# A cross-attention block with a feed-forward layer: the feature order of the key/value input, and the order of the first loads

## The chip, the cores and the metric

The kernel runs on one core of one Trainium2 chip. The metric is the time of one execution on the device, in microseconds (us). Before the change three runs gave 788.25 us as the median (787.9 to 791.28).

The engines are called by their names in the profile: PE (TensorE, matmuls; PEld is its loading of weights), DVE (VectorE), ACT (ScalarE), POOL (GpSimd) and SP (SyncE, which here only issues transfers). A name with a q (SPq, ACTq, POOLq) is the engine's instruction queue, where it waits and issues.

## The reference

For each of 16 batches `b`, with `x[b]` and `ctx[b]` both 128 x 1024 in float32:

```
h   = layernorm(x)
Q   = h @ Wq + bq                 # 1024 x 1024, 32 heads of 32
K   = ctx @ Wk + bk               # 1024 x 256, 8 heads of 32
V   = ctx @ Wv + bv               # 1024 x 256
w   = softmax(Q K^T / sqrt(32))   # 4 query heads share one key/value head
x   = x + (w V) @ Wo + bo
x   = x + scale * (ei(layernorm(x)) @ kernel)   # 1024 x 1024, entries 0 or 1; ei scales the last 205 features by -4
```

The change concerns K and V alone: sums over the 1024 features of `ctx` with `Wk` and `Wv`. The order in which these features are summed is free, as long as `ctx` and the weights use the same one.

## The kernel before

The batches go in 8 groups of two (`GB = 2`). PE multiplies with 128 features at a time on the partitions, so each operand is cut into `NC = 8` chunks of 128 features. The weights `Wv` and `Wk` (each 1024 x 256, 1 MB) are read once into `wv_sb` and `wk_sb`, laid out as [partition, chunk, column]. `Wq` and `Wo` come again and again in pieces of 512 KB.

`ctx[b]` comes with rows on the partitions and is wanted with features on the partitions. DVE's transpose (`turn_ctx`, line 349) turns blocks of 32 x 32 only, so `load_ctx` (line 152) makes four transfers of 128 KB per batch: transfer k puts features 256k to 256k+255 of all 128 rows on the 32 partitions 32k to 32k+31, in runs of 1 KB, four per partition. Two transposes of 128 x 512 elements then give the two halves of `cT`: the first half has chunks 0 to 3, the second 4 to 7. Before the change feature 256k + 32c + f stands on partition 32k + f of chunk c, and a transpose reads its 32 x 32 blocks as 32 adjacent elements of a partition. `load_by_quadrants` (line 161) brings the weights in the same order: one transfer per quadrant of 32 partitions and per cut of chunks, in runs of 1 KB (one row of 256 columns): 12 for `Wv` (cuts at chunks 2 and 4), 8 for `Wk` (a cut at 4).

The transfers of the start are dealt round-robin to three issuing engines (SP, ACT, POOL) in the order `ctx0`, `Wv`, `ctx1`, `Wk`; then SP alone issues `x0`, `x1` (line 169), `bo` (line 201) and the first eight pieces of `Wq` (line 225). The tile framework gives the transfers of SP and ACT eight completion semaphores in turn, so that a transfer waits in its queue until the one issued eight before it has landed.

The order of the work is written out by hand on the host: a `Stream` holds generators of PE work, and a list of later events. In the first stage, PE's order is `v` of batch 0, `v` of batch 1 (`prep_v`, 16 matmul records each), `k` of both (`prep_k`, 32), the transposes of the normalized `x` (`tp_x`), then the plain `q` product. DVE's order is: two transposes of `ctx0`, two of `ctx1`, the two additions `v + bv` (line 412), `bqs` (line 852), and `norm_x(0)`, `norm_x(1)`: two `bn_stats` each (line 283), their aggregate, a power on POOL (line 291) and one scaling (line 292). An engine's instructions run strictly in order.

In the next stage (group 0's attention with the preparation of group 1) DVE also has the softmax (row maxima L580, division L596), sums of pieces of `Wq` (L790), the transposes of the next group's `ctx` (L349), its normalizations and `v` additions. PE needs from it above all `cT` for `k` and the divided `p` for its transposes `tpp` (L601). From group 1 on `x` too goes through DVE's transposes (L371), and the output projection's partial sums are read by DVE (L676) before PE may go on in their PSUM buffer. In each later group four transposes of `ctx` are due.

Of the kernel before, what the change touches and what calls it, by code (L numbers as in the profile page):

```python
# [9 lines left out]
FP = mybir.dt.float32  # L10
# [7 lines left out]
P = 128  # L18
# [64 lines left out]
def kernel(  # L83
# [16 lines left out]
    nc = tc.nc  # L100
# [7 lines left out]
    NC = D // P  # L108
    XB = 3
    TB = 4  # L110
    GB = 2
# [9 lines left out]
    work = ctx.enter_context(tc.tile_pool(name="work", bufs=1))  # L121
# [8 lines left out]
    wk_sb = const.tile([P, NC, KV], FP, name="wk_sb")  # L130
    wv_sb = const.tile([P, NC, KV], FP, name="wv_sb")
# [13 lines left out]
    NB = P // 32  # L145

    def load_ctx(b, queues=(nc.sync,)):
        c_t = work.tile([P, NB, NC, 32], FP, tag="ctx", name=f"ctx{b}", bufs=2)
        src = key_value[b].rearrange("(t r) (k c f) -> k r t (c f)", r=32, k=NB, c=NC)
        for k in range(NB):  # L150
            dst = c_t[k * 32 : (k + 1) * 32].rearrange("r t c f -> r t (c f)")
            queues[k % len(queues)].dma_start(out=dst, in_=src[k])
        cs[b] = c_t

    def load_by_quadrants(dst, w, queues, *cuts):

        src = w.rearrange("(k c f) n -> k f c n", k=NB, f=32)
        n = 0
        for lo, hi in zip((0,) + cuts, cuts + (NC,)):
            for k in range(NB):  # L160
                queues[n % len(queues)].dma_start(
                    out=dst[k * 32 : (k + 1) * 32, lo:hi], in_=src[k][:, lo:hi]
                )
                n += 1

    def load_x(b, tag="row"):

        x_t = work.tile([P, D], FP, tag=tag, name=f"xn{b}", bufs=2)
        nc.sync.dma_start(out=x_t, in_=x[b])
        xns[b] = x_t  # L170
# [10 lines left out]
            )  # L181

    three = (nc.sync, nc.scalar, nc.gpsimd)
    load_ctx(0, three)
    load_by_quadrants(wv_sb, Wv, (nc.scalar, nc.gpsimd, nc.sync), 2, 4)
    load_ctx(1, three)
    load_by_quadrants(wk_sb, Wk, (nc.scalar, nc.gpsimd, nc.sync), 4)
    load_x(0)  # L190
    load_x(1)
    ident = const.tile([P, P], FP, name="ident")
    make_identity(nc, ident)
# [88 lines left out]
    def half_stats(stats, src, k):  # L282
        nc.vector.bn_stats(stats[:, k], src[:, k * HALF : (k + 1) * HALF])

    def normalize(dst, src, stats, name):
        mv = small.tile([P, 2], FP, tag="mv", name=f"mv_{name}")
        nc.vector.bn_aggr(mv, stats)
        ve = small.tile([P, 1], FP, tag="ve", name=f"ve_{name}")
        nc.vector.tensor_scalar_add(ve, mv[:, 1:2], EPS)
        rstd = small.tile([P, 1], FP, tag="rstd", name=f"rs_{name}")  # L290
        nc.gpsimd.tensor_tensor(rstd, ve, minus_half, ALU.pow)
        nc.vector.tensor_scalar(dst, src, mv[:, 0:1], rstd, ALU.subtract, ALU.mult)
# [24 lines left out]
    def new_stats(name):  # L317
        return small.tile([P, D // HALF, 6], FP, tag="stats", name=f"st_{name}")
# [9 lines left out]
    HC = NC // 2  # L328
# [15 lines left out]
    def turn_ctx(b, h):  # L344
        grp, j = b // GB, b % GB
        if (grp, h) not in cTs:
            cTs[grp, h] = work.tile([P, HC, T], FP, tag="tT", name=f"cT{grp}_{h}", bufs=TB)
        src = cs.pop(b) if h == 1 else cs[b]
        nc.vector.transpose(  # L349
            cTs[grp, h][:, :, j * S : (j + 1) * S].rearrange("p c (t n) -> p t c n", t=NB),  # L350
            src[:, :, h * HC : (h + 1) * HC],
        )

    rows = {}
# [21 lines left out]
    def prep_ctx(grp, *us):  # L376

        for n, at in enumerate(us if grp < NGRP else ()):
            stream.later(at, lambda n=n: turn_ctx(grp * GB + n % GB, n // GB))
# [7 lines left out]
    def norm_x(b):  # L387
        stats = new_stats(f"a{b}")
        for k in range(D // HALF):
            half_stats(stats, xns[b], k)  # L390
        normalize(xns[b], xns[b], stats, f"a{b}")
# [432 lines left out]
    with tc.manual_schedule():  # L824
        stream = Stream()
# [18 lines left out]
        for j in range(GB):  # L844
            for h in range(2):
                turn_ctx(j, h)
            stream.add(prep_v(0, [j]))
        stream.add(prep_k(0))
        for j in range(GB):
            load_ctx(GB + j)  # L850
        stream.run(0.0, lambda: len(stream.queue) > 1)
        nc.vector.tensor_scalar_mul(bqs, bqT, scale)
        for j in range(GB):
            norm_x(j)

        def sums_of_wo():
            def inputs():
# [57 lines left out]
        for grp in range(NGRP):  # L915
# [5 lines left out]
            if first:  # L921
                stream.add(
                    once(prep_ctx, nxt, 12.5, 13.5),
                    between(plain(1), 9, sums_of_wq, 0),
                    once(sums_of_wq, 1),
                    once(turn_ctx, nxt * GB, 1),
                    once(turn_ctx, nxt * GB + 1, 1),
                    once(norms, nxt, 5.0, 10.0),
# [33 lines left out]
            if not more:  # L962
                for q in range(2 * NA):
                    b, a = grp * GB + q % GB, q // GB
# [6 lines left out]
            for q in range(2 * NA):  # L971
                b, a = grp * GB + q % GB, q // GB
# [66 lines left out]
```

## Time and profile before

| | |
|---|---|
| median of 3 runs | 788.25 us |
| profiled execution, its time | 788.44 us |
| its span in the profile | 786.7 us |
| PE busy | 767.2 us (98%) |
| DVE, ACT, POOL busy | 486.3, 322.4, 112.2 us |
| mean share of 16 DMA engines, slices of the first 255 us | 0.6 to 0.9 and more |
| transposes of `ctx`, L349 | 32 of 699 ns, 22.1 us |
| steady groups | one every 93.8 us |

The span runs from the first instruction to the last; 1.8 us of the time lie outside it. The chain that ended last is PE for 88% of the span, DVE for 4%, DMA for 2%. In the windows of 94 us from 151 us to 621 us PE is busy for all of each window, so what happens on the other engines there shows in the time only if PE comes to wait. The waits that PE has are few and lie in the first 150 us; the prediction shows them.

In a row of the timeline the columns are start, duration, engine, line, operation, written and read tile, count of merged instructions, and in brackets the idle time before the first with what ended it. In a row of the stage table they are the stage and its length, then busy time and count of instructions for PE, PEld, DVE, ACT and POOL, granted clock of PE, share of the DMA engines and GB/s (or PE's alone, where that engine was asked for). A matmul's record counts its pass through the array, which overlaps the next one's.

### The profile page before, as it was taken

To read this page: it belongs to the slowest core of one execution; us is meant where nothing else is said; L and a number is where in the kernel's file an instruction comes from. 1 tells how busy PE (TensorE), PEld (TensorE's weight loads), DVE (VectorE), ACT (ScalarE), POOL (GpSimd) and SP (SyncE) were. 2 spreads that over 40 slices of the span, in tenths; PEclk is the share of its full clock that TensorE was granted. 3 is DMA by queue.
4 is the path that set the end of the run, shared out by engine and by line. 5 is a ranking of instruction groups with operands and counts; after the bars stand their busy time and mean duration, and the time that the engine had idled before them with its cause. 6 is when DMAs were issued, how large, how long until landed. Compare 5 with 4: busy or idle time off the path is not lost.

```text
span 786.7 us, 13740 instructions
## 1 busy us (share of the span) xinstructions
PE 767.2 (98%) x5008; PEld 571.6 (73%) x5008; DVE 486.3 (62%) x886; ACT 322.4 (41%) x1261; POOL 112.2 (14%) x142
## 2 busy tenths in 40 slices
PE   5998999999999999999999999999999999999997
PEld 4886884589746997479864898558984699556476
DVE  2158647756766567566774667856676666765552
ACT  0254764444334443344433444334434445575100
POOL 4154703020010102010020200202001010103000
PEclk9999999999999999999999999999999999999999
DMA  9999799988698776978778785987869657763802
GB/s 248 344 309 303 273 341 392 268 226 282 216 322 230 238 235 232 306 204 261 239 240 271 213 272 188 305 257 202 266 209 328 206 192 238 250 202 104 264 27 81
DMA packets 99268, 192.42 MB, mean 245 GB/s; under 512 B 8240, under 2 KB 57456, under 8 KB 99200
## 3 DMA queue, kind: packets, MB, share of 16 engines
q1 hardware_dynamic: 97568, 189.43, 74.9%
q0 software_dynamic: 528, 1.12, 0.6%
q10 hardware_dynamic: 1104, 0.98, 0.6%
q8 instruction: 40, 0.66, 0.3%
q14 instruction: 28, 0.23, 0.1%
HBM read 161.09 MB, written 30.41 MB: 243 GB/s over the span
## 4 chain that ended last, share of the span: by engine, by line
PE 88%; DVE 4%; DMA 2%; issue 2%; ACT 1%; POOL 1%; SPq 0%; POOLq 0%; DVEq 0%
PE f L323 14%; PE o_u L662 13%; PE q_u L451 12%; PE o_v L662 7%; PE tpp L601 7%; PE q_v L451 6%; PE k L323 6%; PE v L323 6%; PE sc L568 4%; PE av L611 4%; PE q L323 3%; PE o_c L662 3%; PE q_c L451 3%; DVE p L596 1%; DMA piece<-o 1%
## 5 line engine op out<-in xcount | busy, mean ns | idle before, releaser
L584 ACT ACTIVATE p<-sc,negm 128x128 f32<-128x128 f32 x512 | 181.1, 368 | 134.4 <-DVE negm L580 72.5
L603 ACT COPY pt<-tpp 128x512 f32<-128x512 f32 x128 | 74.6, 591 | 148.1 <-PE tpp L601 147.9
L580 DVE TENSOR_REDUCE negm<-sc 128x4 f32<-128x512 f32 x128 | 86.8, 680 | 59.3 <-PE sc L568 59.3
L584 ACT ACTIVATION_READ_ACCUMULATOR p<-sc,negm 128x1 f32 x512 | 105.5, 206 | 0.0
L323 PE MATMUL f<-wf_sb,x2l 128*128 128x512 f32 x256 | 104.3, 408 | 0.0
L323 PE MATMUL f<-wf_sb,x2h 128*128 128x512 f32 x256 | 100.5, 393 | 0.0
L596 DVE TENSOR_TENSOR p<-p,inv 128x512 f32<-128x512 f32 x128 | 90.9, 710 | 4.4
L451 PE MATMUL q_u<-t,piece 128*128 128x128 f32 x672 | 81.3, 275 | 0.0
L601 PEld LDWEIGHTS tpp<-ident,p 128*128 128x128 f32 x512 | 62.2, 141 | 24.9 <-issue 16.8
L601 PE MATMUL tpp<-ident,p 128*128 128x128 f32 x512 | 76.4, 274 | 3.7 <-DVE p L596 3.5
L451 PEld LDWEIGHTS q_u<-t,piece 128*128 128x128 f32 x672 | 78.0, 192 | 0.1
L180 POOL TENSOR_TENSOR x<-x,bo_b 128x256 f32<-128x256 f32 x64 | 53.6, 862 | 155.7 <-DMA x<-in_x_dram 155.7
L323 PE MATMUL v<-wv_sb,cT 128*128 128x256 f32 x256 | 62.2, 393 | 9.0 <-DMA wv_sb<-in_L_xattn_Wv_dram 7.1
L662 PE MATMUL o_v<-piece,s 128*128 128x512 f32 x128 | 60.3, 598 | 0.5 <-DVE x L676 0.5
L323 PEld LDWEIGHTS v<-wv_sb,cT 128*128 128x128 f32 x256 | 48.4, 197 | 15.8 <-DVE cT L349 9.4
L662 PE MATMUL o_u<-piece,s 128*128 128x512 f32 x128 | 59.2, 594 | 0.6 <-DVE x L676 0.6
L323 PE MATMUL k<-cT,wk_sb 128*128 128x256 f32 x256 | 58.3, 380 | 1.0 <-DVE cT L349 1.0
L662 PE MATMUL o_u<-piece,yT 128*128 128x512 f32 x128 | 58.6, 599 | 0.0
L323 PEld LDWEIGHTS f<-wf_sb,x2l 128*128 128x128 f32 x256 | 48.2, 188 | 10.6 <-issue 1.1
L323 PEld LDWEIGHTS k<-cT,wk_sb 128*128 128x128 f32 x256 | 47.9, 190 | 10.2 <-issue 2.6
L323 PEld LDWEIGHTS f<-wf_sb,x2h 128*128 128x128 f32 x256 | 48.2, 188 | 9.6 <-issue 0.5
L568 PEld LDWEIGHTS sc<-kT,qT 32*128 32x128 f32 x1024 | 31.4, 186 | 25.8 <-issue 25.8
(86 smaller groups left out, 935.1 us busy)
## 6 DMA issues: line engine op xcount, KB each, us to landing
piece<-o SPq DMA_DIRECT2D x64, 512.0 KB, 5.0
piece<-q SPq DMA_DIRECT2D x56, 512.0 KB, 5.1
piece<-in_L_xattn_Wq_dram SPq DMA_DIRECT2D x50, 512.0 KB, 5.2
piece<-in_L_xattn_Wo_dram SPq DMA_DIRECT2D x48, 512.0 KB, 4.6
xn<-in_x_dram SPq DMA_DIRECT2D x16, 512.0 KB, 6.8
x<-in_x_dram SPq DMA_DIRECT2D x16, 512.0 KB, 4.6
ctx<-in_ctx_dram SPq DMA_DIRECT2D x60, 128.0 KB, 6.6
out_dram<-x SPq DMA_DIRECT2D x15, 512.0 KB, 2.7
```

Source lines behind the costliest of these rows:

```text
L180: lambda cut=cut: nc.gpsimd.tensor_add(x_t[:, cut], x_t[:, cut], bo_b[:, cut]) and None,
L323: nc.tensor.matmul(mm, lhsT=lhsT, rhs=rhs, start=k == 0, stop=k == n - 1)
L451: nc.tensor.matmul(mm if part is None else mm[:, part], lhsT=lhsT, rhs=rhs, start=start and n == k == 0, stop=k == len(some) - 1, skip_gro ...
L568: nc.tensor.matmul(tiles[i][:, g], lhsT=qT[rows, g], rhs=kT[rows, a, cols], start=True, stop=True,)
L580: nc.vector.tensor_reduce(negm, tile_, AX.X, ALU.max, negate=True)
L584: nc.scalar.activation(p[:, g], tile_[:, g], AF.Exp, bias=negm[:, g : g + 1], accum_out=total[:, g : g + 1],)
L596: nc.vector.tensor_mul(p, p, inv.unsqueeze(2).to_broadcast([P, NG, S]))
L601: nc.tensor.transpose(tp[:, g], p[:, g], ident)
L603: nc.scalar.copy(pt, tp)
L611: nc.tensor.matmul(mm[i * HD : (i + 1) * HD], lhsT=vs[b][:, h * HD : (h + 1) * HD], rhs=pts[i], start=True, stop=True,)
L662: nc.tensor.matmul(mm, lhsT=lhsT[:, 2 * k + c], rhs=w[:, c], start=start and k == c == 0, stop=k == c == 1, skip_group_check=True,)
```

## The change

The features of K's and V's input are taken in another order: feature 8p + c stands on partition p in chunk c. The four transfers of `ctx` per batch bring the same bytes to the same places as before; what differs is how the transpose reads them: its 32 elements of a block now lie 8 elements (32 bytes) apart in the partition. It writes what it wrote before. In the weights, the eight rows 8p to 8p+7 of a partition are now adjacent in memory: each matrix comes in two transfers, one on SP and one on ACT, each to all 128 partitions in runs of 4 KB (four chunks).

`ctx0` and `ctx1` are issued by SP and ACT alone; POOL issues no large transfer of the start any more. `x0` is loaded in front of `Wk`, `x1` stays behind it. On DVE, `norm_x(0)` moves between the two `v` additions, `norm_x(1)` follows the second, and `bqs` comes last. PE's order is the same instruction for instruction.

```diff
     def load_ctx(b, queues=(nc.sync,)):
-        c_t = work.tile([P, NB, NC, 32], FP, tag="ctx", name=f"ctx{b}", bufs=2)
-        src = key_value[b].rearrange("(t r) (k c f) -> k r t (c f)", r=32, k=NB, c=NC)
+        c_t = work.tile([P, NB, 32, NC], FP, tag="ctx", name=f"ctx{b}", bufs=2)
+        src = key_value[b].rearrange("(t r) (k n) -> k r t n", r=32, k=NB)
         for k in range(NB):
-            dst = c_t[k * 32 : (k + 1) * 32].rearrange("r t c f -> r t (c f)")
+            dst = c_t[k * 32 : (k + 1) * 32].rearrange("r t f c -> r t (f c)")
             queues[k % len(queues)].dma_start(out=dst, in_=src[k])
...
-    def load_by_quadrants(dst, w, queues, *cuts):
-        src = w.rearrange("(k c f) n -> k f c n", k=NB, f=32)
...
+    def load_rows(dst, w, queues):
+        src = w.rearrange("(p c) n -> p c n", p=P)
+        for h in range(2):
+            cut = slice(h * NC // 2, (h + 1) * NC // 2)
+            queues[h].dma_start(out=dst[:, cut], in_=src[:, cut])
...
-    three = (nc.sync, nc.scalar, nc.gpsimd)
-    load_ctx(0, three)
-    load_by_quadrants(wv_sb, Wv, (nc.scalar, nc.gpsimd, nc.sync), 2, 4)
-    load_ctx(1, three)
-    load_by_quadrants(wk_sb, Wk, (nc.scalar, nc.gpsimd, nc.sync), 4)
+    two = (nc.sync, nc.scalar)
+    load_ctx(0, two)
+    load_rows(wv_sb, Wv, two)
+    load_ctx(1, two)
     load_x(0)
+    load_rows(wk_sb, Wk, two)
     load_x(1)
...
             cTs[grp, h][:, :, j * S : (j + 1) * S].rearrange("p c (t n) -> p t c n", t=NB),
-            src[:, :, h * HC : (h + 1) * HC],
+            src[:, :, :, h * HC : (h + 1) * HC].rearrange("p t f c -> p t c f"),
...
-        stream.run(0.0, lambda: len(stream.queue) > 1)
+        stream.run(0.0, lambda: len(stream.queue) > 2)
+        norm_x(0)
+        stream.run(stream.now, lambda: len(stream.queue) > 1)
+        norm_x(1)
         nc.vector.tensor_scalar_mul(bqs, bqT, scale)
-        for j in range(GB):
-            norm_x(j)
```

More of the change, by code (lines that the diff above doesn't have):

```diff
@@ L147, in load_ctx @@
     def load_ctx(b, queues=(nc.sync,)):
-        c_t = work.tile([P, NB, NC, 32], FP, tag="ctx", name=f"ctx{b}", bufs=2)
-        src = key_value[b].rearrange("(t r) (k c f) -> k r t (c f)", r=32, k=NB, c=NC)
+        c_t = work.tile([P, NB, 32, NC], FP, tag="ctx", name=f"ctx{b}", bufs=2)
+        src = key_value[b].rearrange("(t r) (k n) -> k r t n", r=32, k=NB)
         for k in range(NB):
-            dst = c_t[k * 32 : (k + 1) * 32].rearrange("r t c f -> r t (c f)")
+            dst = c_t[k * 32 : (k + 1) * 32].rearrange("r t f c -> r t (f c)")
             queues[k % len(queues)].dma_start(out=dst, in_=src[k])
         cs[b] = c_t
-    def load_by_quadrants(dst, w, queues, *cuts):
-        src = w.rearrange("(k c f) n -> k f c n", k=NB, f=32)
[L158 to L164, printed above, removed]
+    def load_rows(dst, w, queues):
[3 more added lines that the diff above has]
+            queues[h].dma_start(out=dst[:, cut], in_=src[:, cut])
     def load_x(b, tag="row"):
```

## The prediction

> **What bounds the kernel now.** I read PE's waits first, over the whole run, because PE is busy for 767.2 of 786.7 us:
>
> ```profile
> PE v L323 <- DMA wv_sb<-in_L_xattn_Wv_dram: 7.1, 1, 7.1
> PE tpp L601 <- DVE p L596: 3.5, 3, 2.7
> PE v L323 <- DVE cT L349: 1.9, 1, 1.9
> PE k L323 <- DVE cT L349: 1.0, 1, 1.0
> PE o_u L662 <- DVE x L676: 0.6, 1, 0.6
> PE o_v L662 <- DVE x L676: 0.5, 1, 0.5
> ```
>
> The columns are total, times, longest. Two waits belong to the start (7.1 and 1.9), the others to DVE. Then the timeline, to place them:
>
> ```profile
> 5.91 1.30 DVE L349 STREAM_TRANSPOSE cT<-ctx 128x512 f32<-128x512 f32 x2 [5.91 <-DMA ctx<-in_ctx_dram]
> 7.06 5.51 PE L323 MATMUL v<-wv_sb,cT 128*128 128x256 f32 x16 [7.06 <-DMA wv_sb<-in_L_xattn_Wv_dram]
> 13.73 1.30 DVE L349 STREAM_TRANSPOSE cT<-ctx 128x512 f32<-128x512 f32 x2 [6.51 <-DMA ctx<-in_ctx_dram]
> 14.50 3.72 PE L323 MATMUL v<-wv_sb,cT 128*128 128x256 f32 x16 [1.92 <-DVE cT L349]
> 18.05 7.07 PE L323 MATMUL k<-cT,wk_sb 128*128 128x256 f32 x32
> 27.22 13.98 PE L323 MATMUL q<-xT,piece 128*128 128x256 f32 x64
> ...
> 61.74 1.29 DVE L349 STREAM_TRANSPOSE cT<-ctx 128x512 f32<-128x512 f32 x2
> 63.08 5.45 PE L323 MATMUL k<-cT,wk_sb 128*128 128x256 f32 x24 [0.99 <-DVE cT L349]
> 77.81 1.22 DVE L596 TENSOR_TENSOR p<-p,inv 128x512 f32<-128x512 f32 x1
> 79.18 1.09 PE L601 MATMUL tpp<-ident,p 128*128 128x128 f32 x4 [2.66 <-DVE p L596]
> ...
> 136.81 1.98 PE L662 MATMUL o_u<-piece,s 128*128 128x512 f32 x4 [0.58 <-DVE x L676]
> 141.91 1.98 PE L662 MATMUL o_v<-piece,s 128*128 128x512 f32 x4 [0.53 <-DVE x L676]
> ```
>
> The reader is to see three places. At the start PE waits for data: `Wv` until 7.06, `ctx1` until 14.50. From about 54 to 79 us and from 125 to 143 us DVE runs almost without a gap, and PE waits for its results. Everywhere else PE sets the end. The stage table gives the transfer rates:
>
> ```profile
> 2.00:4.00 2.00, 0.00 (x0) 0.00 (x0) 0.00 (x0) 0.00 (x0) 2.00 (x5) 1.00 1.03 251
> 18.00:20.00 2.00, 2.00 (x12) 1.74 (x11) 1.71 (x5) 0.00 (x0) 0.00 (x0) 1.00 1.01 392
> 22.00:24.00 2.00, 2.00 (x11) 1.77 (x10) 1.50 (x4) 0.18 (x1) 0.35 (x1) 1.00 1.10 348
> ```
>
> The DMA engines are full in all three. `ctx`, `Wv`, `Wk` (32 partitions, 1 KB) move at 251 GB/s, `Wq` (128 partitions, also 1 KB) at 348, `x` and `bo` (128 partitions, 4 KB) at 392. So the spread over partitions is worth more than the length of the run.
>
> **The start: what it gains.** The bytes in front of the first matmul are `ctx0` (0.52 MB) and, since the two halves of `Wv` now run abreast on two queues, all of `Wv` (1.05 MB); before, a quarter was enough. Transfers begin to move at 2.0 us (6 GB/s before it). 0.52 MB at 251 take 2.1 us, 1.05 MB at 348 to 392 take 3.0 to 2.7, some 0.2 for landing: `Wv` is there at about 7.2. `ctx0`'s first transpose has been done by then even if it takes 1.2 us (4.3 + 1.2). All at 392 gives 6.0; nothing faster than 251 gives 8.3. So the first matmul comes at 7.2 (6.0 to 8.3), no earlier than the 7.06 of before.
>
> From there v, v and k run without a gap if the rest lands. Before, the two v took from 7.06 to 18.22, with 1.92 idle: 9.24 of work. So they end at 7.2 + 9.24 = 16.4 instead of 18.2: 1.8 us gained (3.0 to 0.7). Covers: `ctx1` lands at 2.0 + 4.2 + 3.0 + 0.2 = 9.4 and its transpose takes 1.2, due at 12.7: 2 us of cover. `x0` and `Wk` (1.57 MB at 370) land by 13.7, `k` is due at 16.4: 2.7 us of cover; at 251 they would be 0.4 late. `x1` lands at about 15.0.
>
> Why the first v takes 5.51 and the second 3.72 decides whether that 9.24 shrinks:
>
> ```profile
> 8.50:9.50 1.00, 1.00 (x4) 1.00 1.08 257
> 16.50:17.50 1.00, 1.00 (x6) 1.00 1.03 414
> 76.00:82.00 6.00, 3.34 (x15) 2.14 (x17) 3.00 (x4) 0.58 (x1) 5.93 (x7) 0.73 1.05 313
> ```
>
> In the first v evenly spaced matmuls come at 0.43 us, later at 0.22, with no wait recorded between them; and around 79 us, where PE idled for 2.66, the granted clock is 0.73. I read the start as a slow clock too (the table prints 1.00 there, but the spacing is double) and keep the 5.51. The Trainium skill, page "TensorE: Matmul & The Clock Gate", Part 1, has the array at half rate until it has been busy for a window of some 3.4 us; by it the gain stays 1.8, while if the spacing were waits for cuts of `Wv` it would be 3.6.
>
> **Moved and removed, at no cost.** POOL loses nine issues (0.53 to 0.72 us each, some 5 us until 6.7), and its small loads, of which `bkT` is first needed at 21.7, come earlier. In front of the first piece of `Wq` SP has 9 transfers instead of 13, ACT issues 6 instead of 9; SP's waits for the eighth-last landing fall on transfers that are done by then. `norm_x(0)` in front of the second `v` addition waits for `x0` (13.7) with that addition, `norm_x(1)` and `bqs` behind it. The first v ends at 12.7, so its addition is done by 13.1; `norm_x` takes 3.3 us (18.67 to 21.94), ends at 17.0, and the second addition, due at 16.4, waits 0.6. Nobody waits for that before the attention of batch 1. `norm_x(1)` ends at 20.7, needed at 16.4 + 6.9 = 23.3. Pieces 0 and 1 of `Wq` land by 19.4, `q` starts at 25.4: 6.0 us of cover. Without these covers each item would cost its own lateness, at most 1 to 3 us.
>
> **The transposes: what they cost.** L349 reads 32 elements 32 bytes apart instead of adjacent. No row of the trace has such a read, so I bound it. 699 ns is what the transposes take now, and L371 and L728 take 700 and 704 in two other block orders: lower end 0, since there is nothing to make a read faster. The longest row of DVE for 512 elements is one L790 of 1758 ns: upper end +1.06 each. Between them I take the rows where DVE's operand stream is held up, by POOL working beside it: the L596 above, 1.22 instead of 0.69, and an L507 of 1.21 instead of 0.68. That is +0.53, the middle of the bounds as well.
>
> What the page "Vector Engine (DVE) Microarchitecture Reference" of the Trainium skill says in "Measured stream behaviour on trn2 (trn3 not measured)" speaks against this change: a port keeps its rate only if elements come in pairs of adjacent 4-byte words; single words far apart took 1.73 ns per column instead of 1.05, some with short steps 2.5. By it a transpose would cost 0.35 to 0.74 more (my estimate), the sum below +0.7 to +3.4; by the equal rows of L349, L371 and L728 alone it would be -1.8.
>
> Where it counts: 32 transposes. Four at the start are covered as above. Four stand in the first full stretch of DVE (two at 56.46, two at 61.74), in front of the row maxima that ACT waits for, and so of everything up to 79.18: 4 x 0.53 = 2.1 us on the path. Four stand in the second stretch (125.75, 130.96, 137.48, 141.77); two are in front of the wait at 136.81, a third in front of that at 141.91: 3 x 0.53 = 1.6 us. Those of later groups are covered: the one at 294.94 has its next division done at 297.58 and PE's `tpp` not before 299.25, 1.7 us of cover; the other three of that group come after the softmax's last division. Both stretches start from something that PE releases, so the gain of the start carries into them.
>
> **Sum.** -1.8 + 2.1 + 1.6 = +1.9 on the profiled 788.44, or with the 0.2 that the median lies below it: 790.1 us.
>
> **Rivals.**
> Transposes as fast as before: only -1.8 stays, 786.4 (787.5 to 785.2). For it: three block orders at one duration. Against it: none of them steps within a block.
> Slower, by the transposes alone: at +0.82 each, 7 x 0.82 - 1.8 = 3.9 us, over 0.5%. It decides earlier if PE's longer idling (0.99 at 63 us grows to 3) brings the slow clock a second time: the 0.73 over 6 us costs 1.6 us, and the point is +0.59. At the upper end 788.25 - 1.8 + 7.4 + 1.6 = 795.5. For it: both stretches of DVE are really full.
> The weights come no faster (8.3 for the first matmul): gain 0.7, 788.25 - 0.7 + 3.7 = 791.3. Against it: the 392 of `x` and `bo`.
> Faster by over 0.5%: the first v shrinks to 3.72 (1.8 more) and the first matmul comes at 6.0: 3.0 + 1.8 = 4.8, transposes unchanged: 783.5. It needs three ends at once.
>
> **Numbers.** The forecast has 0.40 (own range 788 to 792.2), the unchanged transposes 0.15, the slower side 0.31, slow weights 0.05, faster 0.09. 0.5% is 3.9 us, about what a measurement of this kernel can tell from no change. Slower: 0.31, and 0.05 from the edges of the forecast and of slow weights; faster: 0.09 and 0.03 from unchanged transposes with the best start; the same: 0.52. The range reaches from the unchanged transposes to the upper end of the slower side, 785.2 to 795.5.
>
> **What would show it.** The mean of L349 (right: 1.1 to 1.4 us; 0.70 is the first rival). First v at 7.2, no idle in front of the second, `q` at 25.4. PE's waits near 63 and 79 us together about 2 us longer, those near 137 and 142 together 1.6 longer. The first v in 3.7 us, or PE waiting for `Wk` or `xn`, makes the start wrong; PE waiting for `cT` or `p` after 200 us makes the cover wrong.

## The result, and the profile after

| | before | after |
|---|---|---|
| median, 8 runs each | 788.80 us (787.23 to 791.28) | 791.68 us (789.81 to 793.18) |
| ratio, with its 95% interval | | 1.0032 [1.0022, 1.0043] |
| profiled execution, time and span | 788.44, 786.7 us | 793.18, 791.4 us |

The change costs 2.9 us, 0.3%, and the interval lies wholly above 1. The profiled execution after is the slowest of its eight, 1.5 us above their median, so not every delay in its trace is the kernel's rule; the second profile of the same kernel (e5 below) starts `k` 1.0 us earlier.

In the profile after, the transposes are line 344, the products of `k` and `v` line 318, `tpp` line 596, the softmax's division line 591, the read of the partial sums line 671. PE's waits (total, times, longest):

```profile
PE v L318 <- DMA wv_sb<-in_L_xattn_Wv_dram: 11.6, 1, 11.6
PE tpp L596 <- DVE p L591: 3.5, 3, 2.7
PE k L318 <- DVE cT L344: 2.0, 1, 2.0
PE o_u L657 <- DVE x L671: 1.4, 1, 1.4
PE o_v L657 <- DVE x L671: 0.9, 1, 0.9
```

The wait for `ctx1` inside `v` (1.9 before) is gone. But the first wait has grown from 7.1 to 11.6, and the three waits for DVE from 1.0, 0.6 and 0.5 to 2.0, 1.4 and 0.9. That for `p` has not moved. The timeline of PE and DVE after, with the start first:

```profile
5.40 2.06 DVE L344 STREAM_TRANSPOSE cT<-ctx 128x512 f32<-128x512 f32 x2 [5.40 <-DMA ctx<-in_ctx_dram]
11.64 8.88 PE L318 MATMUL v<-wv_sb,cT 128*128 128x256 f32 x32 [11.64 <-DMA wv_sb<-in_L_xattn_Wv_dram]
14.98 2.10 DVE L344 STREAM_TRANSPOSE cT<-ctx 128x512 f32<-128x512 f32 x2 [7.51 <-DMA ctx<-in_ctx_dram]
20.35 7.07 PE L318 MATMUL k<-cT,wk_sb 128*128 128x256 f32 x32
29.52 1.68 PE L318 MATMUL q<-xT,piece 128*128 128x256 f32 x7
...
66.37 5.45 PE L318 MATMUL k<-cT,wk_sb 128*128 128x256 f32 x24 [1.98 <-DVE cT L344]
82.46 0.63 PE L596 MATMUL tpp<-ident,p 128*128 128x128 f32 x4 [2.65 <-DVE p L591]
...
140.89 1.98 PE L657 MATMUL o_u<-piece,s 128*128 128x512 f32 x4 [1.39 <-DVE x L671]
146.40 1.98 PE L657 MATMUL o_v<-piece,s 128*128 128x512 f32 x4 [0.94 <-DVE x L671]
```

Subtract the starts of before from these: `k` is 2.3 us late (20.35 against 18.05), the `k` of the next stage 3.29, `tpp` 3.28, `o_u` 4.08, `o_v` 4.49, and the span ends 4.7 later. So this execution lost 2.3 at the start, and then 1.0, 0.8 and 0.4 at the three places at which PE waits for a transposed tile or for a DVE that is late because of one. The transposes themselves, in the list of costliest groups (busy us, mean ns, and DVE's idle time before them):

```profile
L344 DVE STREAM_TRANSPOSE cT<-ctx 128x512 f32<-128x512 f32 x32 | 36.1, 1137 | 12.9 <-DMA ctx<-in_ctx_dram 12.9
L723 DVE STREAM_TRANSPOSE turn_f<-turn_f 128x512 f32<-128x512 f32 x28 | 19.7, 704 | 0.0
L366 DVE STREAM_TRANSPOSE xT<-turn_x 128x512 f32<-128x512 f32 x24 | 16.7, 700 | 0.0
```

Same shape, same type, in one run: 1137 ns with a read that steps by 32 bytes, 700 and 704 with adjacent elements.

### The profile page after: what moved, and what is told of

It is laid out like the page before. It is cut to its first block, busy times and chain, and to the rows that moved or that the text cites. A ratio compares the mean times of both kernels' runs of the same rounds, so it can differ in the third digit from the quotient of the medians.

```text
span 791.4 us, 13716 instructions
## 1 busy us (share of the span) xinstructions
PE 767.0 (97%) x5008; PEld 571.4 (72%) x5008; DVE 498.9 (63%) x886; ACT 322.4 (41%) x1261; POOL 107.0 (14%) x133
## 4 chain that ended last, share of the span: by engine, by line
PE 85%; DMA 7%; DVE 3%; SPq 2%; POOL 1%; issue 1%; ACT 0%; DVEq 0%; POOLq 0%
PE f L318 14%; PE o_u L657 13%; PE q_u L446 13%; PE o_v L657 7%; PE tpp L596 7%; PE q_v L446 6%; PE v L318 5%; PE k L318 5%; PE sc L563 4%; PE av L606 4%; PE q_c L446 3%; PE o_c L657 3%; DMA ctx<-in_ctx_dram 2%; DMA wo<-in_L_xattn_Wo_dram 2%; SPq L220 1%; DMA o<-wo 1%
## 5 line engine op out<-in xcount | busy, mean ns | idle before, releaser
L318 PE MATMUL v<-wv_sb,cT 128*128 128x256 f32 x256 | 61.4, 390 | 11.6 <-DMA wv_sb<-in_L_xattn_Wv_dram 11.6
L318 PEld LDWEIGHTS v<-wv_sb,cT 128*128 128x128 f32 x256 | 48.2, 195 | 17.7 <-issue 11.6
```

The costliest lines, as they stand in the source:

```text
L318: nc.tensor.matmul(mm, lhsT=lhsT, rhs=rhs, start=k == 0, stop=k == n - 1)
```

## Experiments

The ratios below are each against the kernel before, run on the same chip beside it.

| run | what | ratio [95%] | first matmul | `k` starts |
|---|---|---|---|---|
| after | the change | 1.0032 [1.0022, 1.0043] | 11.64 | 20.35 |
| e5 | the change, once more | 1.0032 [1.0019, 1.0044] | 10.20 | 19.33 |
| e2 | order of features alone, queues of before | 1.0025 [1.0014, 1.0035] | 7.46 | 19.04 |
| e3 | loads alone, adjacent reads | 1.0004 [0.9993, 1.0016] | 9.26 | 18.51 |
| e13 | strided reads from group 3 on | 1.0000 [0.9987, 1.0013] | 8.18 | 17.10 |
| e1 | small loads later | 1.0018 [1.0008, 1.0028] | 9.26 | 18.18 |
| e7 | rows of `x` behind `Wk` again | 1.0038 [1.0026, 1.0051] | 9.51 | 19.41 |
| e6 | `Wv` in four transfers | 1.0036 [1.0024, 1.0049] | 8.68 | 19.84 |
| e9 | `ctx1` held back | 1.0096 [1.0080, 1.0111] | 8.73 | 24.08 |
| e10 | all behind `Wv` held back | 1.0053 [1.0037, 1.0069] | 8.56 | 19.62 |
| e4 | pairs | 0.9981 [0.9968, 0.9994] | 8.23 | 17.69 |
| e11 | pairs, once more | 1.0005 [0.9994, 1.0015] | 10.05 | 19.05 |
| e12 | pairs, `ctx1` inside `Wv` | 0.9999 [0.9985, 1.0013] | 8.99 | 18.17 |

### The two halves of the change apart

**e2: the order of features alone.** Queues, cuts and quadrants of before; only which feature stands where, and so the transpose's read (and the weights' runs in memory, which grow to 2 and 4 KB).

```diff
...
-        src = w.rearrange("(k c f) n -> k f c n", k=NB, f=32)
+        src = w.rearrange("(k f c) n -> k f c n", k=NB, f=32)
...
-            src[:, :, h * HC : (h + 1) * HC],
+            src[:, :, :, h * HC : (h + 1) * HC].rearrange("p t f c -> p t c f"),
```

> The kernel before, with the feature order 8p + c alone: weights still by quadrants of 32 partitions over three queues in the same cuts (their runs grow to 2 and 4 KB), strided reads in the transposes, loads and norms in the old places. If the transposes alone cost what PE's waits show (0.99 near 63 us, 0.81 and 0.41 near 137 and 142), the time is 788.8 + 2.2 = 791.0 and the first matmul stays near 7 us. If the strided read is harmless and the changed start is the whole loss: 788 to 789.5.

It took 1.0025 of before, +2.0 us, with transposes of 1135 ns. PE's waits for DVE, in the list of waits:

```profile
PE v L323 <- DVE cT L349: 9.5, 2, 7.5
PE k L323 <- DVE cT L349: 2.0, 1, 2.0
PE o_u L662 <- DVE x L676: 1.4, 1, 1.4
PE o_v L662 <- DVE x L676: 0.9, 1, 0.9
```

The last three are the waits of after, with the queues and cuts of before. The first belongs to the start: here PE's first matmul (7.46) waits for the slower transpose instead of `Wv`, and `k` comes at 19.04, 1.0 us later than in the one profile of before. The order of features alone makes most of the loss.

**e3: the loads alone.** The transposes read 32 adjacent elements again, while loads, queues and norms stay changed. K and V are then not the reference's, since `ctx` and the weights no longer use the same order; the amount of work is the same.

```diff
-            src[:, :, :, h * HC : (h + 1) * HC].rearrange("p t f c -> p t c f"),
+            src.rearrange("p t f c -> p t (f c)").rearrange("p t (c f) -> p t c f", c=NC)[:, :, h * HC : (h + 1) * HC],
```

> The changed kernel, but its transposes read 32 adjacent elements as before the change, so that ctx and the weights are in different feature orders and K and V are not the reference's; all loads, queues and counts stay. It leaves the start of the change alone. If the transposes cost 2.2 us on the path: 791.7 - 2.2 = 789.5, L344 at 0.70 us, PE's waits near 66, 141 and 146 us back at 1.0, 0.6 and 0.5; what is then left over the 788.8 of before (0.7) is the start's loss. By the prediction's own start (1.8 gained) it would be 787.0. If the transposes are harmless: 791.7.

```profile
PE v L318 <- DMA wv_sb<-in_L_xattn_Wv_dram: 9.3, 1, 9.3
PE tpp L596 <- DVE p L591: 3.5, 3, 2.7
PE k L318 <- DVE cT L344: 1.0, 1, 1.0
PE o_u L657 <- DVE x L671: 0.6, 1, 0.6
PE o_v L657 <- DVE x L671: 0.5, 1, 0.5
```

The three waits are those of before to a tenth, and the time is too: 1.0004. So the new loads are worth nothing, where 1.8 us had been forecast. The first wait says why: 9.3 where 7.2 was forecast.

**e13: strided reads where they should be hidden.** Groups 0 to 2 read adjacent elements, groups 3 to 7 keep the strided read. K and V of groups 0 to 2 are not the reference's.

```diff
-            src[:, :, :, h * HC : (h + 1) * HC].rearrange("p t f c -> p t c f"),
+            src[:, :, :, h * HC : (h + 1) * HC].rearrange("p t f c -> p t c f")
+            if grp > 2
+            else src.rearrange("p t f c -> p t (f c)").rearrange("p t (c f) -> p t c f", c=NC)[:, :, h * HC : (h + 1) * HC],
```

> The changed kernel with the transposes of groups 0 to 2 reading adjacent elements and those of groups 3 to 7 the strided ones; K and V of groups 0 to 2 are then not the reference's. Theory (the slower transposes of the steady groups lie behind PE): time as with all of them adjacent, 0.999 to 1.0015 of the kernel before, no wait of PE for a transpose or a division after 150 us, the waits near 63 and 137 us back at 1.0 and 0.6. Rival (each of 20 transposes costs part of its 0.43 us): 1.003 or more, with such waits after 200 us.

```profile
L344 DVE STREAM_TRANSPOSE cT<-ctx 128x512 f32<-128x512 f32 x32 | 31.2, 986 | 10.3 <-DMA ctx<-in_ctx_dram 10.3
```

DVE is busy with this group for 9.1 us more than before (31.2 against the 22.1 of L349), all of it on 20 transposes, and the time is 1.0000. PE waits 1.0, 0.6 and 0.5 for DVE, and for no transpose after 150 us; for a division it waits once, 0.42 us near 721 us, as in the kernel before. The loss comes from the twelve transposes of the first three groups, of which four stand at the start.

### Why the first matmul is late

**e1: the small loads later.** A suspicion: POOL's four small loads are now among the first transfers, and their packets could hold the weights up. They go behind `Wk` on ACT's queue instead.

```diff
-    nc.gpsimd.dma_start(out=bkT, in_=bk)
+    nc.scalar.dma_start(out=bkT, in_=bk)
...
```

> The changed kernel, with the four small loads (bkT, bv_b, bqT, fscale) taken from POOL's queue, where they were issued from 1.3 us on beside Wv, to ACT's queue behind Wk. Theory A (these small loads, served beside Wv, hold some DMA engines up, so that Wv lands at 11.6 instead of 7.2 us): the first matmul comes at 7.2 to 8.5, q at 25.4 to 27, and the time falls by 2 to 4 us against the changed kernel's 791.7, to 788 to 790. Theory B (Wv lands late because its packets of 4 KB on two queues are slow themselves): the first matmul stays at 11 to 12, the time at 791 to 793. Theory C (the profiled execution was an outlier): the first matmul anywhere, the time at 791 to 792.

First matmul at 9.26, the very figure of e3, which has these loads where the change puts them; time 1.0018, with an interval that overlaps those of after and of e2, so that a gain of 1 us can be neither shown nor excluded. The small loads are not what keeps the first matmul from 7.2.

**e5: the changed kernel again.**

> The changed kernel once more, unedited, to see whether its first matmul at 11.64 us belongs to the kernel or to one execution. Theory (that execution was a late one): the first matmul at 8.2 to 9.6, as in the two runs with the same loads that showed 9.26, and a span 1.5 to 4 us below 791.4. Rival (the small loads that POOL issues hold the weights up): 11 to 12 again. Time of both: 1.002 to 1.005 of the kernel before.

First matmul at 10.20, between both expectations, and a span of 789.2 against 791.4. So the 11.64 was one execution's, but 9 to 10 is not an accident. With the same transfers (after, e5, e3, e13) the first matmul came at 11.64, 10.20, 9.26 and 8.18, and never at 7.2. From issue to landing, by the list of transfers, the two halves of `Wv` took, in after and in e13 (KB each, us):

```profile
wv_sb<-in_L_xattn_Wv_dram SPq DMA_DIRECT2D x1, 512.0 KB, 9.9
wv_sb<-in_L_xattn_Wv_dram ACTq DMA_DIRECT2D x1, 512.0 KB, 10.2
```

```profile
wv_sb<-in_L_xattn_Wv_dram SPq DMA_DIRECT2D x1, 512.0 KB, 6.4
wv_sb<-in_L_xattn_Wv_dram ACTq DMA_DIRECT2D x1, 512.0 KB, 6.7
```

**e9 and e10: nothing behind Wv.** The next suspicion: a transfer is spread over all sixteen DMA engines and lands with the last of them, and the transfers issued behind `Wv` keep some engines busy. In e9 a POOL copy of two elements of `Wv` goes into `ctx1`'s buffer ahead of its transfers, so that these wait; in e10 such copies go ahead of all that follows on SP and ACT.

The edit of e9:

```diff
-    def load_ctx(b, queues=(nc.sync,)):
+    def load_ctx(b, queues=(nc.sync,), behind=None):
...
+        if behind is not None:
+            nc.gpsimd.tensor_copy(
+                out=c_t[:, 0, 0, 0:2], in_=behind[:, NC // 2 - 1 : NC // 2 + 1, 0]
+            )
...
-    load_ctx(1, two)
+    load_ctx(1, two, wv_sb)
```

> The changed kernel with the second context's transfers, and all behind them on the two queues, held until both halves of Wv have landed (a POOL copy of two elements of Wv into the context's buffer goes ahead of them). Theory (Wv is late because its engines also carry the second context's 0.52 MB, issued within 3 us of it): Wv lands at 6.9 to 7.8 and the first matmul follows, its sixteen engines ending within 1 us of each other; the second context lands at 10 to 12. Rival (Wv in this form is slow by itself): first matmul still at 8.8 to 9.6. The time is not the point: with the theory 1.000 to 1.003 of the kernel before, since the second context or Wk may come late, with the rival 1.003 to 1.007.

In e9 the first matmul came at 8.73. It tells little: with `ctx1` held, the tile framework issued `x0` and `Wk` at 2.1 to 4.1 in its place, so the engines were as busy as ever, and the second `v` waited 5.0 us for `ctx1` (1.0096).

> The changed kernel with every transfer behind Wv on both queues held until Wv has landed (POOL copies of two elements of Wv into each destination go ahead of them), so that only the first context, Wv and one small load are under way. Theory (the transfers behind Wv delay its last engine): first matmul at 7.0 to 7.9, the sixteen engines ending Wv within 0.6 us of each other. Rival (Wv's rows of 4 KB land late by themselves): first matmul at 8.6 or later, as with x0 and Wk behind it. The time tells nothing here, since the second context comes some 3 us later: 1.005 to 1.012 of the kernel before.

In e10 only `ctx0`, `Wv` and one small load are under way, and the first matmul still comes at 8.56. So sharing with later transfers is not what separates 7.2 from 8.6; whether it adds to the 10.20 and 11.64 of other executions is left open by this run. The stage table of e10 shows what remains (stage, length, busy time and count of PE, PEld, DVE, ACT, POOL, clock, DMA share, GB/s):

```profile
2.00:4.00 2.00, 0.00 (x0) 0.00 (x0) 0.00 (x0) 0.00 (x0) 0.32 (x2) 1.00 1.07 259
4.00:5.00 1.00, 0.00 (x0) 0.00 (x0) 0.00 (x0) 0.00 (x0) 0.00 (x0) 1.00 0.91 194
5.00:7.00 2.00, 0.00 (x0) 0.00 (x0) 1.57 (x2) 0.00 (x0) 0.00 (x0) 1.00 0.99 373
7.00:8.00 1.00, 0.00 (x0) 0.00 (x0) 0.49 (x1) 0.00 (x0) 0.00 (x0) 1.00 0.27 107
8.00:9.00 1.00, 0.43 (x1) 0.47 (x2) 0.00 (x0) 0.00 (x0) 0.34 (x3) 1.00 0.00 0
```

Sum the bytes: 0.52 MB until 4.0 (`ctx0`), then 0.19 + 0.75 + 0.11 = 1.05 MB until 8.0 (`Wv`). The 373 GB/s that the forecast had counted on is there for two microseconds of four. In the first of them the transfers change over at 194 GB/s, and in the last the share is 0.27, the work of some four of sixteen engines, while the others have nothing to do; then comes half a microsecond until the landing is seen. On average 262 GB/s, and a landing 0.5 behind the last byte. This is one profile, and why some engines end last was not tried. Idle engines before the landing show with all transfers under way as well: from 8 to 10 us the share is 0.56 in after and 0.45 in e5.

**e6: Wv in four transfers.** The first matmul then needs a quarter of the bytes.

```diff
-    def load_rows(dst, w, queues):
+    def load_rows(dst, w, queues, parts=2):
...
-        for h in range(2):
-            cut = slice(h * NC // 2, (h + 1) * NC // 2)
-            queues[h].dma_start(out=dst[:, cut], in_=src[:, cut])
+        for h in range(parts):
+            cut = slice(h * NC // parts, (h + 1) * NC // parts)
+            queues[h % 2].dma_start(out=dst[:, cut], in_=src[:, cut])
...
-    load_rows(wv_sb, Wv, two)
+    load_rows(wv_sb, Wv, two, 4)
```

> The changed kernel with Wv in four transfers of two chunks (runs of 2 KB), SP and ACT in turn, in place of two of four chunks; nothing else. Theory (the first matmul waits for the last of sixteen engines to finish a half of Wv, which they share with the transfers behind it): two chunks are a quarter of the bytes, so the first matmul moves from 9.3 to between 6.5 and 7.8, the chunks after it come in time (each takes 0.69 at the slow clock), the second half of v then waits for the second context's transposes if these are still at 12 to 13; v ends 0.5 to 1.5 earlier, time 1.001 to 1.003 of the kernel before. Rival (a transfer's latency, not its bytes): first matmul at 8.8 or later, and time as the changed kernel.

8.68 instead of 6.5 to 7.8, and just short of the rival's 8.8; that a quarter too lands with its slowest engine would fit, but is not shown. The second `v` now waits 1.35 us for `ctx1`, which was issued and landed later. `k` starts at 19.84, the time is 1.0036. Cuts bring nothing back here.

**e7: the first rows behind Wk again,** and both norms behind the last transposes.

```diff
+    load_rows(wk_sb, Wk, two)
     load_x(0)
-    load_rows(wk_sb, Wk, two)
     load_x(1)
...
-        stream.run(0.0, lambda: len(stream.queue) > 2)
-        norm_x(0)
-        stream.run(stream.now, lambda: len(stream.queue) > 1)
-        norm_x(1)
+        stream.run(0.0, lambda: len(stream.queue) > 1)
         nc.vector.tensor_scalar_mul(bqs, bqT, scale)
+        for j in range(GB):
+            norm_x(j)
```

> The changed kernel with the first rows of x loaded behind Wk again, and both norms behind the last transposes as before the change. Theory (the place of the rows is worth nothing, because k ends some 2 us after the norms in every trace): time within 0.1 per cent of the changed kernel, 1.002 to 1.005 of the kernel before, q starting within 0.5 us of 9.1 after k's start. Rival (the rows in front of Wk hide a norm that would come last): q 1 to 2.6 us later against k's start, time 1.004 to 1.007.

`q` starts 9.16 us after `k` (28.57 and 19.41), in e5 9.17. Time 1.0038 beside e5's 1.0032. The place of the rows is worth nothing that these runs can show, as expected.

### A version without the loss

**e4 and e11: pairs.** Feature 16q + 2c + e goes to partition 2q + e, so that two adjacent elements of `ctx` belong to the same chunk and a transpose reads pairs, 64 bytes apart. The weights then come in runs of 1 KB, each matrix in four transfers of 64 partitions.

```diff
-        c_t = work.tile([P, NB, 32, NC], FP, tag="ctx", name=f"ctx{b}", bufs=2)
+        c_t = work.tile([P, NB, 16, NC, 2], FP, tag="ctx", name=f"ctx{b}", bufs=2)
...
-        src = w.rearrange("(p c) n -> p c n", p=P)
+        src = w.rearrange("(q c e) n -> e q c n", c=NC, e=2)
...
-            queues[h].dma_start(out=dst[:, cut], in_=src[:, cut])
+            for e in range(2):
+                queues[e].dma_start(out=dst[e::2, cut], in_=src[e][:, cut])
...
-            src[:, :, :, h * HC : (h + 1) * HC].rearrange("p t f c -> p t c f"),
+            src[:, :, :, h * HC : (h + 1) * HC].rearrange("p t f c e -> p c (t f) e"),
```

> The changed kernel in a third feature order: pairs of features stay adjacent (feature 16q + 2c + e on partition 2q + e of chunk c), so that a transpose reads pairs of adjacent elements; the weights come to all partitions, even ones by SP and odd ones by ACT, in runs of 1 KB, chunks 0 to 3 first. If the cost of the strided read lies in single words, the transposes are back at 0.70 us, and the time is that of the start alone, 789 to 790; with half of Wv enough for the first matmul, which then comes at 6 to 8 us, 787 to 788. If any stride costs, transposes stay at 1.0 to 1.2 us and the time at 790 to 792.

> The version with pairs (feature order 16q + 2c + e on partition 2q + e) once more, unedited, on another chip. Theory (its gain belongs to the version): 0.997 to 0.9995 of the kernel before, span 785 to 787, transposes 0.70. Rival (one lucky set of runs): 0.9995 to 1.002.

The transposes, by their line (ns least, median, most), in e4:

```profile
L345 DVE STREAM_TRANSPOSE cT<-ctx x32: 662/703/711, 5.4 to 589.1; 128x512 f32<-128x512 f32 x32
```

Pairs are read at full speed, and the loss is gone. A gain is not: 0.9981 in seven runs, 1.0005 in twelve others on another chip, and the first matmul at 8.23 and at 10.05. The first set alone would have been taken for a kernel that beats both.

**e12: pairs, with ctx1 issued between the two halves of Wv.**

```diff
-    def load_rows(dst, w, queues):
+    def load_rows(dst, w, queues, halves=(0, 1)):
...
-    load_rows(wv_sb, Wv, two)
+    load_rows(wv_sb, Wv, two, (0,))
     load_ctx(1, two)
+    load_rows(wv_sb, Wv, two, (1,))
     load_x(0)
```

> The version with pairs, with the second context issued between the two halves of Wv. Theory (transfers of a queue land in order of issue when they don't all share the engines at once): first half of Wv lands at 6.3 to 7.2, the second context at 9 to 10.5, v then runs without a gap from 6.5 to 7.3 and ends at 15.8 to 16.6, time 0.995 to 0.998 of the kernel before. Rival (what is issued within a few us shares the engines in whatever order): first matmul before 7.5, but the second half of Wv at 9.5 or later halts the first v, end of v at 17 to 18.2, time 0.997 to 1.000, as the version it is made from.

The first matmul came at 8.99, later than either expectation, though half of `Wv` had been issued alone behind `ctx0`; `k` at 18.17, time 0.9999. No version was found that beats the kernel before.

## Why the prediction was right or wrong

The class "no change that 0.5% can show" held, and the 791.68 us lie inside the forecast's own range (788 to 792.2), 1.6 above its 790.1. That it came so near is partly luck: two terms of the sum were wrong by much the same amount in opposite directions.

**The start: the term that failed.** The step is "0.52 MB at 251 take 2.1 us, 1.05 MB at 348 to 392 take 3.0 to 2.7, some 0.2 for landing: `Wv` is there at about 7.2". e10 measured it undisturbed: 4.0 us instead of 2.7 to 3.0 for `Wv`, 0.5 for landing instead of 0.2, first matmul at 8.56; in the full kernel 8.2 to 11.6. A rate taken from the middle of a long stream of transfers was put on a transfer that stands alone, in which some engines end early and half a microsecond passes before the landing is seen. What adds up to 3 us more in some executions is open. The rival "the weights come no faster" had the nearest first matmul (8.3) and the nearest time (791.3, with the same cost of the transposes), and got 0.05. Nor did the second half of the argument pay: from the first matmul on PE ran without a gap, as forecast, and the 1.9 us that `ctx1` had cost before went into the later start. Gain: 1.8 forecast, nothing measured (the ratios of e3 and e13 are 1.0004 and 1.0000, each known to about 1 us).

**SP's waits** for the eighth-last landing were to "fall on transfers that are done by then". They do not: in after, the half of `Wk` that SP issues (its first four chunks) leaves SP only once `Wv` has landed, after a wait of 5.1 us:

```profile
11.89 0.35 SPq L160 DMA_DIRECT2D wk_sb<-in_L_xattn_Wk_dram  x1
```

`k` starts 8.5 us after this issue and does not wait for it, so the wrong step cost nothing.

**The transposes: right mechanism, size 0.44 instead of 0.53.** 1137 ns is inside the 1.1 to 1.4 that was named, and "as fast as before" is excluded. The 0.53 was the middle of two bounds, backed by rows that another engine had slowed, so that it came this near is luck as well. The Trainium skill's page "Vector Engine (DVE) Microarchitecture Reference", section "Measured stream behaviour on trn2 (trn3 not measured)", gave the direction; as an estimate, the differences of its figures for two-source instructions are 0.68 ns more per column for single words far apart and 1.45 for a short step. The trace has (1137 - 700) / 512 = 0.85 ns, between the two. The page's rule that pairs of adjacent words keep the full rate is what e4 and e11 show, at 0.70 us.

**Where it counts: right places, too much passed on.** For the first full stretch of DVE 4 x 0.53 = 2.1 us were counted; it passed on 1.0. DVE before, in this stretch:

```profile
56.46 1.30 DVE L349 STREAM_TRANSPOSE cT<-ctx 128x512 f32<-128x512 f32 x2
57.68 2.67 DVE L790 TENSOR_TENSOR piece<-piece,piece 128x512 f32<-128x512 f32 x2
61.74 1.29 DVE L349 STREAM_TRANSPOSE cT<-ctx 128x512 f32<-128x512 f32 x2
62.96 1.25 DVE L580 TENSOR_REDUCE negm<-sc 128x4 f32<-128x512 f32 x2
```

and after:

```profile
58.76 2.12 DVE L344 STREAM_TRANSPOSE cT<-ctx 128x512 f32<-128x512 f32 x2
60.80 2.08 DVE L785 TENSOR_TENSOR piece<-piece,piece 128x512 f32<-128x512 f32 x2
64.27 2.05 DVE L344 STREAM_TRANSPOSE cT<-ctx 128x512 f32<-128x512 f32 x2
66.25 1.24 DVE L575 TENSOR_REDUCE negm<-sc 128x4 f32<-128x512 f32 x2
```

The first two transposes took 1.30 us before and take 2.12 now, the second two 1.29 and 2.05: 1.58 more. But the two sums between them fell from 2.67 to 2.08. POOL adds pieces beside them, in both traces from 0.4 us after the first transpose began:

```profile
56.85 2.95 POOL L790 TENSOR_TENSOR piece<-piece,piece 128x512 f32<-128x512 f32 x2 [7.57 <-PE q L323]
```

```profile
59.15 2.58 POOL L785 TENSOR_TENSOR piece<-piece,piece 128x512 f32<-128x512 f32 x2 [11.75 <-PE q L318]
```

Before, POOL's work covered 2.1 us of DVE's slow sums; now DVE is still transposing for most of it and meets POOL for 0.9. That POOL is what slows them is read from this overlap, but it recurs: the same two sums take 2.67 to 2.68 us in e3, e4 and e13, which read adjacent elements or pairs here, and 2.06 to 2.09 in all eight profiles with strided reads in this stretch. So 1.58 - 0.59 = 0.99, which is the growth of the wait at 63 us. The wait at 79 us, forecast to share in it, stayed at 2.65: PE stands behind the same DVE work and had been moved already. The second stretch was counted as 3 x 0.53 = 1.6 and gave 0.81 + 0.41 = 1.2, nearly 3 x 0.44 = 1.3.

**The covers** held. e13 keeps 20 strided transposes from group 3 on and loses nothing, and no run has a wait of PE for `cT` after 200 us. For `p` there is one wait of 0.42 us near 721 us, in before as in after; the part on the time before, which puts all waits into the first 150 us, overlooks it, and it is no sign against the covers. The first `v` kept its slow pace (5.26 us in e10, 5.51 before) as forecast.

**Sum.** Forecast: -1.8 + 2.1 + 1.6 = +1.9. Measured: 0 + 1.0 + 1.2 = +2.2 in waits, and +2.9 in time. Part of the difference is the slow clock of the rival, which was to decide from +0.59 per transpose and shows already at +0.44; the last part estimates it.

## What to carry to other kernels

Price a transfer that gates the first matmul by the time until its last engine ends, read from a transfer that stands alone, not by the rate of a full stream. Before moving a stride from DMA into a DVE read, see whether it can be kept in pairs of adjacent elements: that was the whole difference between 1137 and 700 ns here. And when a kernel lies within 0.3% of another, run it a second time in another set, since the same code gave 0.9981 and 1.0005.

## What was not expected of the hardware

**The clock sets two groups of run times.** Every profile has matmuls at half pace at the start, for some 3 to 6 us from the first one on; the granted clock that the tables print does not cover it. Some have one more such stretch, of 3.4 us, near 65 or near 80 us. PE in tens of microseconds (busy time and count, granted clock, DMA share, GB/s), before and in e3:

```profile
60.00:70.00 10.00, 9.01 (x50) 1.00 0.95 339
70.00:80.00 10.00, 6.90 (x36) 0.94 1.07 279
80.00:90.00 10.00, 9.76 (x94) 0.89 0.50 190
```

```profile
60.00:70.00 10.00, 9.01 (x64) 1.00 1.00 354
70.00:80.00 10.00, 6.91 (x38) 1.00 1.00 265
80.00:90.00 10.00, 9.76 (x104) 1.00 0.53 204
```

PE is busy for the same time and idles for the same 2.66 us in front of 79 us; the clock falls in one and not in the other. In e5 it fell at once after the longer wait for `cT`:

```profile
65.35 7.13 PE L318 MATMUL k<-cT,wk_sb 128*128 128x256 f32 x24 [1.98 <-DVE cT L344]
81.44 0.63 PE L596 MATMUL tpp<-ident,p 128*128 128x128 f32 x4 [1.60 <-DVE p L591]
```

The matmuls of `k` took 7.13 instead of 5.45, and the wait for `p` took 1.05 of the 1.68 back. All eight profiles with strided reads in the first groups have exactly one such stretch between 60 and 90 us, four near 65 us, four behind the wait for `p` (e9 has another near 19 us, behind its wait of 5.0 us). A stretch of 3.4 us at half rate lowers the mean granted clock of 787 us to 0.998. The clock also falls in every profile after PE's last matmul, where it costs nothing; at most 2.4 us of that lie in the span, which alone leave 0.998 to 1.000. So a run at 0.999 or more had no other stretch, and nearly all of those below had one:

| kernels | runs | clock 0.999 or more | their median | median of the others |
|---|---|---|---|---|
| before | 70 | 34 | 787.97 | 789.27 |
| e3, e4, e11, e12, e13 | 55 | 36 | 787.87 | 790.49 |
| strided: after, e1, e2, e5, e6, e7 | 44 | 0 | | 791.25 |

Before, about half of the runs escape it; with the longer waits none does. Strided runs lie 2.0 us above those runs of before that did not escape (791.25 against 789.27), which is about the 2.2 us of waits. As an estimate, 34 of 70 times the 1.3 to 2.6 us between the two medians is 0.6 to 1.3 us, which together with the 2.2 us makes 2.8 to 3.5, around the measured 2.9. The page "TensorE: Matmul & The Clock Gate", Part 1, says that the clock follows windows of some 3.4 us that run on whatever the kernel does, so that where they fall decides; the two cases of one and the same idle time agree with that, and so does e5, where an idle time of 1.98 us was enough. Shifting a kernel on purpose against these windows was not tried.

**A landing is not the last byte.** In e10 the last bytes of `Wv` moved before 8.0 us and PE started at 8.56; and the two halves of one matrix took 6.4 to 10.2 us from issue to landing in kernels whose loads are identical.
